# The last stage of a two-layer graph attention network, its instructions put in another order on TensorE and VectorE

## The chip, the cores and the metric

The kernel runs on one core of a Trainium2 chip. The metric is the device time of one launch in microseconds (us). Three runs of the kernel before took 2143.78, 2143.87 and 2149.99 us; their median is 2143.87 us.

## The reference

Two graph layers over 4096 nodes with 512 features each, with one adjacency matrix. The second layer is itself two rounds of attention and a dense network of two layers:

```python
def heads(x, mask, W, a):
    Wh = einsum('nf,hfo->hno', x, W)
    e = leaky_relu(src[:, :, None] + dst[:, None, :], 0.2)   # src, dst: Wh times the halves of a
    attn = softmax(where(mask, e, NEG), axis=-1)
    return einsum('hnm,hmo->hno', attn, Wh)
...
x = layernorm(x + L0(x, adj))                  # 8 heads of 64
h = elu(heads(x, adj > 0, W1, a1))             # 8 heads of 64
h2 = elu(heads(h, adj > 0, Wo, ao)[0])         # 1 head of 512
out = relu(h2 @ lin1_w + lin1_b)               # 512 -> 1024
x = layernorm(x + out @ lin2_w + lin2_b)       # 1024 -> 512
```

The adjacency is sparse (some 8 neighbours of a node on the mean, many more for the first nodes). The kernel finds the edges, and works on lists of them.

## The kernel before

The work runs in four stages: the edges are found; the attention of layer 0; the first attention of layer 1; and the last stage, which is the second attention of layer 1 together with the dense network, the residual and the norm. The change lies in the last stage alone (from L1404).

Nodes lie in 32 tiles of 128. A tile's edges are cut into chunks of 128, and chunks into units of at most 6 (GC). The last stage has 66 units, called u0 to u65 here in their order. Tiles with few neighbours have one unit or two; tile 0 has eleven (u16 to u26). Tiles are put together in blocks (L1417 to L1421): two tiles in the first block and in the last, four in each of the seven others.

What a unit needs, with the function and lines:

- **gather** (L1067): one indirect DMA for each chunk, issued by GpSimd, brings 128 rows of the table into `g`. Four units' buffers (GT) exist; unit i + 4 is gathered once unit i has been summed.
- **next weights**, `weights` (L1133): three small VectorE operations on the scores (`z`, L1147, L1148, L1150; the first waits for the gather) and an exponential on ScalarE (`w`, L1158).
- **matrices and sums**, `add` (L1160): VectorE makes a 128x64 selection matrix for each slot from `w` (`sm`, L1187), TensorE multiplies by the gathered rows into `acc` (L1212).

What a tile needs:

- **scores**, `spread` (L1078), two tiles ahead: matmuls into `pss` (L1101, L1108), a sum on VectorE (`s`, L1117) and `ls` (L1129). More than 20 chunks make several cuts, all but the last of which are collected at once.
- **the tile's end**: `inverse` (`rd`, L1224), `normal` (`o`, L1239), then `elu`: two ScalarE operations (`ex`, L1247, L1248) and one on VectorE (L1249). In `fold` all of it stands in one place.
- **the turn**, `turn` (L1447): four transposes of `o` on TensorE (L1452), and a ScalarE copy into `sht` (L1453). With the last tile of a block turned, eight dense pieces of the block become ready (four for a block of two tiles).

What a block needs: **dense pieces**. `first_dense` multiplies `sht` by `lin1_w` (L1475) and leaves relu on ScalarE (`shid`, L1478). `second_dense` loads the residual row `xr` on the SP queue (L1483), adds the bias on VectorE (L1484), multiplies `shid` by `lin2_w` (L1487), and leaves the rest for `close`: the residual (L1492), the **norm** on VectorE (L1253 to L1266) with two ScalarE operations in its middle (L1258, L1259), and the store on the SP queue (L1494). `piece` (L1459) takes the next piece from `ready`, after `close`.

The last stage is under `tc.manual_schedule()`: each engine takes its instructions in the order in which the loop emits them, and the loop's order is each engine's order. A piece is due when `due` reaches 1; `due` grows by `pace` for each chunk, so that the pieces of one block are spread over the units of the next. In the loop before, a unit emits, in this order: scores' matmuls of the tile two ahead, the turn of the tile ended one unit earlier, the next unit's weights, the earlier tile's `rd`, matrices and sums, gather, `close`, the tile's end, the scores' rest, due pieces.

Of the kernel before, what the change touches and what calls it, by code (L numbers as in the profile page):

```python
# [10 lines left out]
F32 = mybir.dt.float32  # L11
# [10 lines left out]
P = 128  # L22
N = 4096
F = 512
# [534 lines left out]
def sparse_path(  # L559
# [23 lines left out]
    nc = tc.nc  # L583
# [57 lines left out]
    x1_d = dram.tile([N, F], F32, name="sx1_d")  # L641
# [407 lines left out]
    def units_of(order):  # L1049
        units = []  # L1050
        for t in order:
            own = [
                Unit(t, [(p.first + i, n) for i, n in runs], slots)
                for p in pts if p.t == t for runs, *slots in p.units()
            ]
            own[0].first = own[-1].last = True
            units += own
        return units
# [186 lines left out]
    def elu(sb, o):  # L1245
        ex = sb.tile([P, F], F32, name="ex")
        nc.scalar.activation(ex, o, AF.Relu, scale=-1.0)  # L1247
        nc.scalar.activation(ex, ex, AF.Exp, scale=-1.0)  # L1248
        return lambda: nc.vector.scalar_tensor_tensor(o, ex, -1.0, o, op0=OP.add, op1=OP.max)  # L1249

    def layernorm(sb, y):
        bs = sb.tile([P, 6], F32, name="bs")
        nc.vector.bn_stats(bs, y)  # L1253
        mv = sb.tile([P, 2], F32, name="mv")
        nc.vector.bn_aggr(mv, bs)
        rs = sb.tile([P, 2], F32, name="rstd")
        lg, r = rs[:, 0:1], rs[:, 1:2]
        nc.scalar.activation(lg, mv[:, 1:2], AF.Ln, bias=eps)  # L1258
        nc.scalar.activation(r, lg, AF.Exp, scale=-0.5)  # L1259

        def rest():

            nc.vector.scalar_tensor_tensor(lg, mv[:, 1:2], EPS, r, op0=OP.add, op1=OP.mult)
            nc.vector.scalar_tensor_tensor(lg, lg, -0.5, r, op0=OP.mult, op1=OP.mult)
            nc.vector.scalar_tensor_tensor(r, lg, 1.5, r, op0=OP.add, op1=OP.mult)
            nc.vector.tensor_scalar(y, y, mv[:, 0:1], r, op0=OP.subtract, op1=OP.mult)  # L1266

        return rest
# [87 lines left out]
    with ExitStack() as pools:  # L1356
        big = pools.enter_context(tc.tile_pool(name="eb", bufs=1))
        sb = pools.enter_context(tc.tile_pool(name="es", bufs=2))
# [24 lines left out]
    sb = ctx.enter_context(tc.tile_pool(name="ls", bufs=2, reuse_waits="tile"))  # L1383
# [23 lines left out]
    with tc.tile_pool(name="tg", bufs=GT, side="right", reuse_waits="tile") as gp, \  # L1407
            tc.tile_pool(name="tb", bufs=1, side="right", reuse_waits="tile") as big, \
            tc.tile_pool(name="ta", bufs=2, space=PSUM, reuse_waits="tile") as pacc, \
            tc.tile_pool(name="tp", bufs=1, space=PSUM, reuse_waits="tile") as ps, tc.manual_schedule():  # L1410

        few = NT - 12
        blocks = [[NT - 1, NT - 2], [NT - 3 - i for i in range(NJ)]]
        blocks += [[1 + b, few // 2 - b, few // 2 + 1 + b, few - b] for b in range(few // NJ)]
        blocks.insert(3, [NT - 9, 0, NT - 8, NT - 7])  # L1417
        blocks.append([NT - 10, NT - 11])
        assert sorted(sum(blocks, [])) == list(range(NT))
        order = [t for block in blocks for t in block]  # L1420
        units = units_of(order)  # L1421
        at = Attention(st2, gp, wk, pacc, ps)
        for _ in range(GT):
            nc.gpsimd.memset(gp.tile([P, GC, F + HS], F32, name="g"), 0.0)
        for u in units[:GT]:
            at.gather(u)
        l1w = big.tile([P, FC, HID], F32, name="sl1w")
        nc.sync.dma_start(l1w, lin1_w.rearrange("(c p) o -> p c o", p=P))
        l2w = big.tile([P, HC, F], F32, name="sl2w")
        nc.sync.dma_start(l2w, lin2_w.rearrange("(c p) o -> p c o", p=P))  # L1430
        l1b_r = big.tile([HC, P], F32, name="sl1b_r")
        nc.sync.dma_start(l1b_r, lin1_b.rearrange("(c p) -> c p", p=P))
        l2b = big.tile([P, F], F32, name="sl2b")
        nc.sync.dma_start(l2b, lin2_b.partition_broadcast(P))
        hts, hids, ready, open_ = {}, {}, [], []

        def fold(t):
            o = at.normal(sb, t)
            elu(sb, o)()
            return o  # L1440

        def turn(t, o):
            b = next(b for b, block in enumerate(blocks) if t in block)
            j, nb = blocks[b].index(t), len(blocks[b])
            if j == 0:

                while any(r[1] == b - 2 and r[0] is first_dense for r in ready):  # L1447
                    piece()
                hts[b] = big.tile([P, FC, NB], F32, name="sht", bufs=2)
            pt = ps.tile([P, FC, P], F32, name="pt")  # L1450
            for c in range(FC):
                nc.tensor.transpose(pt[:, c, :], o[:, ts(c, P)], ident)  # L1452
            nc.scalar.copy(hts[b][:, :, ts(j, P)], pt)  # L1453
            if j == nb - 1:
                per = HC // nb
                ready.extend((first_dense, b, range(i * per, (i + 1) * per)) for i in range(nb))
                ready.extend((second_dense, b, i) for i in range(nb))

        def piece():  # L1459
            close()  # L1460
            of, *what = ready.pop(0)
            of(*what)

        def close():
            while open_:
                open_.pop(0)()

        def first_dense(b, ks):
            if 0 in ks:
                hids[b] = big.tile([P, HC, NB], F32, name="shid")  # L1470
            for k in ks:
                n = len(blocks[b]) * P
                p1 = ps.tile([P, NB], F32, name="p1", tag="p", bufs=2)[:, :n]
                for c in range(FC):
                    nc.tensor.matmul(  # L1475
                        p1, l1w[:, c, ts(k, P)], hts[b][:, c, :n], start=(c == 0), stop=(c == FC - 1)
                    )
                nc.scalar.activation(hids[b][:, k, :n], p1, AF.Relu, bias=l1b[:, k : k + 1])  # L1478

        def second_dense(b, j):  # L1480
            t = blocks[b][j]
            xr = sb.tile([P, F], F32, name="xr", bufs=3)
            nc.sync.dma_start(xr, x1_d[ts(t, P), :])  # L1483
            nc.vector.tensor_add(xr, xr, l2b)  # L1484
            p2 = ps.tile([P, F], F32, name="p2", tag="p", bufs=2)
            for k in range(HC):
                nc.tensor.matmul(  # L1487
                    p2, hids[b][:, k, ts(j, P)], l2w[:, k, :], start=(k == 0), stop=(k == HC - 1)
                )

            def rest():
                nc.vector.tensor_add(xr, p2, xr)  # L1492
                layernorm(sb, xr)()
                nc.sync.dma_start(out[ts(t, P), :], xr)  # L1494

            open_.append(rest)

        for t in order[:2]:
            at.spread(t)()
        at.weights(units[0])  # L1500
        l1b = big.tile([P, HC], F32, name="sl1b")
        pb = ps.tile([P, HC], F32, name="pt")
        nc.tensor.transpose(pb, l1b_r, ident[:HC, :HC])
        nc.vector.tensor_copy(l1b, pb)


        pace = {t: 0.0 for t in blocks[0]}
        for last, block in zip(blocks, blocks[1:]):
            chunks = sum(u.n for u in units if u.t in block)
            pace.update((t, 2 * len(last) / chunks) for t in block)  # L1510
        due, folded = 0.0, None
        for i, u in enumerate(units):
            pos = order.index(u.t)
            spread = at.spread(order[pos + 2]) if u.first and pos + 2 < NT else None
            if folded:
                turn(*folded)
                folded = None
            if i + 1 < len(units):
                at.weights(units[i + 1])
            if u.first and pos > 0:  # L1520
                at.inverse(sb, order[pos - 1])
            at.add(u)
            if i + GT < len(units):
                at.gather(units[i + GT])
            close()
            if u.first and pos > 0:
                folded = order[pos - 1], fold(order[pos - 1])
            if spread:
                spread()
            due = min(due + u.n * pace[u.t], 2.5)  # L1530
            while due >= 1 and ready:
                due -= 1
                piece()
        if folded:
            turn(*folded)
        at.inverse(sb, order[-1])
        turn(order[-1], fold(order[-1]))
        while ready:
            piece()
        close()  # L1540
# [56 lines left out]
```

## Time and profile before

| | |
|---|---|
| time of the profiled execution | 2328.89 us (its span 2326.7 us) |
| median of the three runs without a profile | 2143.87 us |
| PE (TensorE) busy | 1776.6 us, 76% |
| DVE (VectorE) busy | 1328.1 us, 57% |
| ACT (ScalarE) busy | 658.9 us, 28% |
| POOL (GpSimd) busy | 1161.8 us, 50% |
| granted TensorE clock, mean | 0.885 |
| first gather of the last stage | 1556.5 us from the span's start |
| first dense piece | 1607.2 us |

The last stage is the last 770 us of the profiled execution. In the profile's rows an engine is named first, then the line, the operation and what it writes and reads; a bracket at the end of a row of the timeline gives the idle time of that engine before it, and who ended it. A float32 matmul is recorded as two passes, so that a piece of eight matmuls is 16 records.

### The profile page before, as it was taken

The page shows a single profiled execution, that of the slowest core. Times are in us where ns is not written, and L with a number is a line of the kernel's source. Part 1 is how long each engine was busy: PE and PEld are TensorE (multiplying, and loading weights), DVE is VectorE, ACT ScalarE, POOL GpSimd, SP SyncE. Part 2 cuts the span into 40 slices and gives each one's busy share as a digit, 9 for nine tenths or more (in the row PEclk, how much of TensorE's full clock was granted, in tenths as well). Part 3 has the DMA queues.
Part 4 walks back from the last instruction along what each step waited for, and adds up shares of the span by engine and source line. Part 5 has one row for each costly group of instructions (what it writes and reads, how often), then busy time and mean ns, then how long its engine had stood idle before and what let it go on. Part 6 is the DMA issues. An engine that isn't in the chain of part 4 may idle for free.

```text
span 2326.7 us, 29282 instructions
## 1 busy us (share of the span) xinstructions
PE 1776.6 (76%) x8987; PEld 1038.4 (45%) x8987; DVE 1328.1 (57%) x3920; ACT 658.9 (28%) x2311; POOL 1161.8 (50%) x1662
## 2 busy tenths in 40 slices
PE   4778776643987775754997767746999898998997
PEld 3555442212665543531665444424445444444444
DVE  6887776744998776733777655733243424334322
ACT  3446776650332211100433221101111111121121
POOL 5424444456556664627556665646355634444300
PEclk9989997866999896875999988877999999999999
DMA  6434665525667775625566665545354524335301
GB/s 222 141 115 159 224 256 207 210 80 163 201 209 219 212 209 144 174 60 145 154 159 170 175 182 145 158 128 143 87 150 131 170 81 148 101 110 151 93 16 52
DMA packets 132589, 351.94 MB, mean 151 GB/s; under 512 B 41922, under 2 KB 42954, under 8 KB 128454
## 3 DMA queue, kind: packets, MB, share of 16 engines
q0 software_dynamic: 74160, 206.25, 33.1%
q1 hardware_dynamic: 58262, 143.72, 17.5%
q8 instruction: 74, 1.21, 0.2%
q14 instruction: 93, 0.76, 0.1%
HBM read 347.31 MB, written 42.24 MB: 167 GB/s over the span
## 4 chain that ended last, share of the span: by engine, by line
PE 36%; DVE 12%; issue 9%; another core or an unknown queue 6%; DMA 3%; POOL 3%; ACT 2%; SPq 0%; DVEq 0%; POOLq 0%; ACTq 0%
PE acc L1212 13%; PE p L1475 9%; PE ph L697 6%; PE p L1487 5%; DVE g L1200 4%; POOL g L1076 3%; DMA g<-table_t,idx 2%; DMA xr<-sx_d 1%; PE pt L683 1%; DVE bs L1253 1%; DVE sm L1179 1%; DVE sm L1187 1%; DVE xr L1492 1%; DVE z L1147 1%
## 5 line engine op out<-in xcount | busy, mean ns | idle before, releaser
L1076 POOL DMA_INDIRECT g<-table_t,idx x927 | 937.4, 1011 | 720.1 <-PE acc L1212 352.9
L1212 PE MATMUL acc<-g,sm 128*64 128x260 f32 (+2 forms) x4068 | 619.9, 424 | 219.9 <-DVE g L1200 100.7
L1212 PEld LDWEIGHTS acc<-g,sm 128*64 128x64 f32 x4068 | 347.9, 150 | 462.7 <-issue 177.8
L697 PE MATMUL ph<-sw_t,xt 128*128 128x264 f32 (+1 forms) x1536 | 408.4, 415 | 82.1 <-ACT xt L686 46.3
L697 PEld LDWEIGHTS ph<-sw_t,xt 128*128 128x128 f32 x1536 | 303.4, 204 | 154.2 <-ACT xt L686 63.0
L1200 DVE TENSOR_TENSOR g<-g,wp 128x2048 f32<-128x2048 f32 (+3 forms) x132 | 349.1, 2645 | 22.8 <-ACT wp L1155 20.2
L884 DVE MAX8 cand<-key 128x8 f32<-128x353 f32 (+55 forms) x467 | 197.3, 449 | 77.7 <-PE key L878 77.1
L1475 PE MATMUL p<-sht,sl1w 128*128 128x512 f32 (+1 forms) x576 | 229.3, 553 | 2.2 <-issue 1.2
L1487 PE MATMUL p<-sl2w,shid 128*128 128x512 f32 x512 | 227.0, 598 | 0.0
L686 ACT ACTIVATE xt<-pt 128x128 f32<-128x128 f32 x384 | 101.1, 278 | 286.5 <-PE pt L683 132.3
L710 ACT COPY hrow<-ph 128x260 f32<-128x260 f32 (+2 forms) x194 | 71.1, 373 | 311.1 <-PE ph L697 146.2
L1475 PEld LDWEIGHTS p<-sht,sl1w 128*128 128x128 f32 x576 | 107.6, 191 | 114.0 <-issue 108.7
L1487 PEld LDWEIGHTS p<-sl2w,shid 128*128 128x128 f32 x512 | 95.4, 190 | 120.1 <-issue 119.3
L1249 DVE SCALAR_TENSOR_TENSOR o<-ex,o 128x512 f32<-128x512 f32 x64 | 44.4, 694 | 182.8 <-ACT ex L1248 145.1
L877 PE MATMUL key<-sg,s_identb 128*128 128x512 bf16 (+1 forms) x258 | 111.6, 434 | 15.4 <-DVE cand L884 10.1
L848 ACT ACTIVATE sg<-raw 128x4096 bf16<-128x4096 int32 (+1 forms) x39 | 116.9, 2998 | 6.6 <-DMA raw<-in_adj_dram 3.7
L1478 ACT ACTIVATE shid<-p,sl1b 128x512 f32<-128x512 f32 (+1 forms) x72 | 46.0, 639 | 249.5 <-PE p L1475 212.0
L878 PE MATMUL key<-frac,places 128*128 128x512 bf16 (+1 forms) x258 | 111.1, 431 | 2.7 <-POOL places L784 2.7
L1187 DVE TENSOR_SCALAR sm<-iota_n,nl,w 128x64 f32<-128x64 f32 x339 | 83.1, 328 | 31.9 <-ACT w L1158 31.1
L1147 DVE TENSOR_TENSOR z<-s,g 128x16 f32<-128x16 f32 (+9 forms) x291 | 43.6, 174 | 92.0 <-DMA g<-table_t,idx 83.7
L1117 DVE TENSOR_REDUCE s<-pss 128x48 f32<-128x144 f32 (+21 forms) x108 | 32.1, 298 | 102.3 <-remote 55.1
L686 ACT ACTIVATION_READ_ACCUMULATOR xt<-pt 128x1 f32 x384 | 79.7, 208 | 0.0
(185 smaller groups left out, 1811.3 us busy)
## 6 DMA issues: line engine op xcount, KB each, us to landing
raw<-in_adj_dram SPq DMA_DIRECT2D x31, 2048.0 KB
table_t<-hrow SPq DMA_DIRECT2D x64, 260.0 KB
xr<-in_x_dram SPq DMA_DIRECT2D x64, 256.0 KB
g<-table_t,idx POOLq DMA_INDIRECT x927
table_t<-hrow SPq DMA_DIRECT2D x32, 257.0 KB
sx_d<-o SPq DMA_DIRECT2D x32, 256.0 KB
xr<-sx_d SPq DMA_DIRECT2D x32, 256.0 KB
out_dram<-xr SPq DMA_DIRECT2D x32, 256.0 KB
```

What stands on the lines that cost most here:

```text
L686: nc.scalar.activation(xt[:, c, :], pt[:, c, :], AF.Copy, accum_out=st.xparts[:, c, t : t + 1])
L697: nc.tensor.matmul(ph[:n], columns(c), st.w[:, c, j], start=(c == 0), stop=(c == FC - 1))
L848: nc.scalar.activation(sg[:, ts(i, w)], raw[:, ts(i, w)], AF.Sign)
L877: nc.tensor.matmul(out_, ident_b, sg[:, j:e], start=True, stop=False)
L878: nc.tensor.matmul(out_, places[:, w], frac[:, j - w * KW : e - w * KW], start=False, stop=True)
L884: nc.vector.max(out=cand[:, at : at + 8], in_=part)
L1076: nc.gpsimd.indirect_dma_start(out=u.g[:, k, : self.st.row], out_offset=None, in_=self.st.table[:, :], in_offset=bass.IndirectOffsetOnAxis ...
L1187: nc.vector.tensor_scalar(sm[:, at + i], of_g, node[k], u.w[:, k], op0=OP.is_equal, op1=OP.mult)
L1200: nc.vector.tensor_mul(body, body, wp[:, :, :, None].to_broadcast(body.shape))
L1212: nc.tensor.matmul(out_[g * HN : (g + 1) * HN], sm[:, slot], rows(k), start=start, stop=stop)
L1475: nc.tensor.matmul(p1, l1w[:, c, ts(k, P)], hts[b][:, c, :n], start=(c == 0), stop=(c == FC - 1))
L1487: nc.tensor.matmul(p2, hids[b][:, k, ts(j, P)], l2w[:, k, :], start=(k == 0), stop=(k == HC - 1))
```

## The change

Only the loop and the helpers of the last stage are changed; the same instructions are issued, in another order. A unit now emits: scores' matmuls; one due piece; matrices and sums; gather; the scores' rest; the turn of the tile ended one unit earlier; the earlier tile's `rd`, `o` and the two ScalarE steps of `elu`; `close`; the next unit's weights; the VectorE step of `elu`; further due pieces. `due` grows at the unit's start. A residual row is loaded when the piece before it is taken, by `rows_of`.

```diff
+            if ready and ready[0][0] is second_dense:
+                rows_of(*ready[0][1:])
             of(*what)
+
+        def rows_of(b, j):
+            t = blocks[b][j]
+            if t not in resid:
+                resid[t] = sb.tile([P, F], F32, name="xr", bufs=3)
+                nc.sync.dma_start(resid[t], x1_d[ts(t, P), :])
...
         def second_dense(b, j):
             t = blocks[b][j]
-            xr = sb.tile([P, F], F32, name="xr", bufs=3)
-            nc.sync.dma_start(xr, x1_d[ts(t, P), :])
+            rows_of(b, j)
+            xr = resid.pop(t)
...
             spread = at.spread(order[pos + 2]) if u.first and pos + 2 < NT else None
-            if folded:
-                turn(*folded)
-                folded = None
-            if i + 1 < len(units):
-                at.weights(units[i + 1])
-            if u.first and pos > 0:
-                at.inverse(sb, order[pos - 1])
+            due = min(due + u.n * pace[u.t], 2.5)
+            if due >= 1 and ready:
+                due -= 1
+                piece()
             at.add(u)
             if i + GT < len(units):
                 at.gather(units[i + GT])
-            close()
-            if u.first and pos > 0:
-                folded = order[pos - 1], fold(order[pos - 1])
             if spread:
                 spread()
-            due = min(due + u.n * pace[u.t], 2.5)
+            if folded:
+                turn(*folded.pop(0))
+            last, rest = units[i - 1].t if u.first and i else None, None
+            if last is not None:
+                at.inverse(sb, last)
+                o = at.normal(sb, last)
+                rest = elu(sb, o)
+            close()
+            if i + 1 < len(units):
+                at.weights(units[i + 1])
+            if rest:
+                rest()
+                folded.append((last, o))
             while due >= 1 and ready:
                 due -= 1
                 piece()
-        if folded:
-            turn(*folded)
-        at.inverse(sb, order[-1])
-        turn(order[-1], fold(order[-1]))
+        last = order[-1]
+        at.inverse(sb, last)
+        o = at.normal(sb, last)
+        elu(sb, o)()
+        for what in folded + [(last, o)]:
+            turn(*what)
```

How it stands on TensorE where the fifth block's last tile (tile 19, u36 and u37) gives way to the next block's first (tile 3, u38 to u40), read from the order of the two programs' instructions:

```
before: turn of 12, sums u37, dense | scores, sums u38 | turn of 19, sums u39, dense
after:  dense, sums u37, turn of 12 | scores, sums u38 | sums u39, turn of 19, dense
```

Units whose sums follow the sums of the unit before with no dense piece between them, from u7 on: before 7, 10, 14, 19, 21, 23, 25, 27, 30, 35, 39, 48, 57, 65; after 7, 9, 13, 16, 18, 20, 22, 24, 26, 29, 30, 34, 38, 39, 47, 48, 56, 57, 64, 65. The last tile of a block is turned in u3, u7, u16, u30, u39, u48, u57 and u65, before and after; after, the turn stands behind that unit's sums, and the block's first dense piece directly behind the turn.

More of the change, by code (lines that the diff above doesn't have):

```diff
@@ L1434, in sparse_path @@
         nc.sync.dma_start(l2b, lin2_b.partition_broadcast(P))
[L1435 to L1440, printed above, removed]
+        hts, hids, resid, ready, open_ = {}, {}, {}, [], []
         def turn(t, o):
@@ L1510, in sparse_path @@
             pace.update((t, 2 * len(last) / chunks) for t in block)
-        due, folded = 0.0, None
+        due, folded = 0.0, []
         for i, u in enumerate(units):
```

## The prediction

> **What bounds the kernel now.** I read the page's slices first, then the busy time by stretches, the waits of the last stage, and the timeline. The slices (58 us each) show the last stage from the 27th on:
>
> ```profile
> PE   4778776643987775754997767746999898998997
> PEclk9989997866999896875999988877999999999999
> ```
>
> TensorE is filled to eight or nine tenths there, at a granted clock of nine tenths. The busy time by stretches narrows it (length, then PE, PEld, DVE, ACT, POOL, clock, DMA share, GB/s):
>
> ```profile
> 1660.00:1720.00 60.00, 59.74 (x228) 29.89 (x226) 16.93 (x70) 9.47 (x20) 29.09 (x30) 0.97 0.41 114
> 1900.00:1960.00 60.00, 50.91 (x214) 24.57 (x212) 26.37 (x96) 8.44 (x23) 26.10 (x27) 0.97 0.41 120
> ```
>
> The first stretch, with a piece in nearly every unit, is full; the second, with units that have none (u34, u38), loses 9 us in 60, and DVE is under half busy. So the stage is worth TensorE's work plus its holes, and only holes can be won or lost. The timeline shows a typical one (u47 and u48, tile 18 ending a block):
>
> ```profile
> 2042.31 0.96 DVE L1187 TENSOR_SCALAR sm<-iota_n,nl,w 128x64 f32<-128x64 f32 x4
> ...
> 2043.04 2.02 PE L1212 MATMUL acc<-g,sm 128*64 128x257 f32 x16
> 2043.19 0.69 DVE L1492 TENSOR_TENSOR xr<-p,xr 128x512 f32<-128x512 f32 x1
> ...
> 2046.47 0.74 DVE L1239 TENSOR_SCALAR o<-acc,rd 128x512 f32<-128x512 f32 x1
> ...
> 2047.24 0.63 ACT L1247 ACTIVATE ex<-o 128x512 f32<-128x512 f32 x1 [1.86 <-DVE o L1239]
> ...
> 2048.57 0.69 DVE L1249 SCALAR_TENSOR_TENSOR o<-ex,o 128x512 f32<-128x512 f32 x1 [1.36 <-ACT ex L1248]
> ...
> 2049.31 1.05 PE L1452 MATMUL pt<-s_ident,o 128*128 128x128 f32 x4 [4.26 <-issue]
> ...
> 2050.43 3.35 PE L1212 MATMUL acc<-g,sm 128*64 128x257 f32 x16
> ```
>
> With no piece left, TensorE waits 4.26 us for the turn of `o`, which on VectorE stands behind a whole norm. Then the turn takes 1.05 (0.60 elsewhere) and the sums 3.35 (1.95 elsewhere). The stage's start is different; there the gathers rule:
>
> ```profile
> 1572.05 0.17 DVE L1147 TENSOR_TENSOR z<-s,g 128x5 f32<-128x5 f32 x1 [5.95 <-DMA g<-table_t,idx]
> ...
> 1572.90 5.85 PE L1212 MATMUL acc<-g,sm 128*64 128x257 f32 x24 [21.02 <-DMA g<-table_t,idx]
> ```
>
> VectorE waits for u1's gather before it makes the matrices of u0, whose scores were ready at 1565.40. Last, one line of the waits:
>
> ```profile
> DVE xr L1484 <- DMA xr<-sx_d: 56.1, 17, 5.5
> ```
>
> **What the Trainium skill says.** "TensorE: Matmul & The Clock Gate", Part 1 (the HAM clock gate): TensorE falls to half clock after an idle window of some 3.4 us and recovers after as long a busy one. The trace agrees in size: after holes of 3.65 us the turn ran at a granted 0.50, and 24 passes of sums took 5.4 us for 2.82; but a hole of 2.42 also brought 0.61, and one of 2.55 nothing. The same page (engine queue depths) has ScalarE and VectorE strictly in order; the trace fits, with `ex` at 1634.26 queued behind four `shid`, a copy and `w`, although `o` was done at 1627.54. "Perfetto Trace Analysis" (Tensor Engine Instruction) says that a matmul's end is an estimate. Here `rd` at 1835.4 waited for sums whose record ends at 1832.1: true ends can be 3 us later.
>
> **The change part by part.** Prices, all from the timeline of before: piece 7.0 on PE (16 passes of 0.436); sums of a 4-chunk unit 1.95, of a 6-chunk unit 2.82, at half clock some 4.0 and 5.4; turn 0.6, its copy starting 0.64 after the turn and holding ACT 0.48; matrices: first sums 0.36 after their start, 0.98 or 1.43 in all; norm from the last matmul: 0.20, then 1.67 to the mean and variance, ACT 0.56, three small operations 0.6, the last 0.47; weights 0.65, `w` 0.25; `rd` and `o` 0.95, both `ex` 1.31, elu's end 0.6; scores' rest 0.4.
>
> Same instructions, so TensorE's work is unchanged. Where a piece precedes the sums (most units), its 7.0 us cover the chain from one unit's sums to the next: the longest is some 8.5 (worked out below) against 2.82 + 0.6 + 0.3 + 7.0 = 10.7, so moving it costs nothing there; without the piece it costs what follows.
>
> *Uncovered units.* The next weights now stand at the unit's end, behind turn copy (ACT), norm and tile's end. Take u38, from the end of u37's piece: sums u37 to 1.95, turn and scores to 2.85. The copy holds ACT from 2.59 to 3.07; only then come the norm's two operations (mean ready at 1.87): to 3.63; norm done 4.70, weights 5.35, `w` 5.60, first sums 5.96. Hole 3.1, where before had 1.45. The added wait is the copy's: queued behind it are the norm's operations and `w`, and VectorE and TensorE wait for those. Then u39, from u38's sums: matrices done 0.62, rest 1.02, `o` 1.97, `ex` 3.31, elu's end 3.9, sums 4.27, against 1.95 of work: 2.3, mostly hidden if the clock is halved. Last, the piece right behind the turn waits for the copy: 0.7. Together 6.4; before this place lost 8.8 (1.45 + 4.25 in holes, 3.1 in slow passes).
>
> The same working gives, in us lost after / before: u7 8.3 / 8.2; u29 and u30 11.6 / 6.9 (one-unit tiles: copy, both `ex`, norm and `w` in a row make 8.46 to the sums, hole 4.8, then 2.3 and two slow sums); u34 and u35 4.6 / 6.5 (3.1, and 60% of a cold start of 2.5); u38, u39 6.4 / 8.8; u47, u48 6.4 / 6.1; u56, u57 6.4 / 7.5; u64, u65 6.5 / 3.6. New holes: u13 4.7 / 0 (norm, weights, elu to 5.1 against sums of 1.95, then the same), u16 8.0 / 0 (4.8, cold 2.5, copy 0.7), u18 1.3 / 0. In tile 0, u24 and u26 4.8 / 11.0 (before: 2.42 and 3.42 in holes, 5.2 in slow passes; u9, u20, u22 are free, 2.3 against 2.8). Its scores' cuts 3.0 / 5.1 (no matrices to wait for behind them). Tail: 3.8 / 5.3. Short waits of sums on matrices elsewhere, before, 5.6 (five of 0.4 to 1.2, and first passes at 134 for 106 ns); after, none.
>
> Sums: after 75.8, before 74.6: **1.2 us lost**.
>
> *Loading rows early* (SP queue): DVE's 56 us at L1484 vanish. The load moves past no store that it needs; the store before it waits for VectorE either way, three buffers serve. That gain is in the short waits and 1 us of the tail already; the rest was idle beside a running piece.
>
> *The start.* u0's sums no longer wait for u1's gather, and so on for each: one gather of six chunks, 6 x 1.30 = 7.8 us, earlier to the first piece. GpSimd issues without a break there, so nothing else is late at once. Bounds: 0, if what delayed the first turn's copy (done on PE at 1584.0, on ACT at 1598.3, released by nothing that the trace names) comes back; 15, as the gather of u3 would allow a first piece at some 1592 against 1607.2. I take 7.8. Scaled by 2143.87 / 2328.89 = 0.92, as issue seems slower under the profile: 7.2. Holes of TensorE I carry over one to one.
>
> Net: 2328.9 - 7.8 + 1.2 = 2322.3 for a profiled execution, 2143.9 - 7.2 + 1.2 = **2138** for the median.
>
> **The rivals.** *Slower.* True ends of matmuls are late. The new chains pass through TensorE's end (copy) and its last piece (norm) before the next sums, which the old order avoided by having `w` a unit ahead. With 2 us (the trace has 1.5, `rd` at 1705.7 behind a record's end at 1704.2, and 3.3 at 1835.4) at eight places (u7, u13, u16, u29, u34, u38, u47, u56) it is 16 us: 2138 + 16 = 2154. It decides once it costs more than 5.9 / 8 = 0.7 us a place. For it: these two waits; against: ordinary copies start 0.04 us after the record's end. *Faster.* The start yields its 15 us (14 scaled), and half the holes, 3.1 us being below the skill's window, don't cool the clock (five of 2 us, half of them): 2143.9 - 14 + 1.2 - 5 = 2126. For it: the hole of 2.55; against: that of 2.42. *No gain at the start*: the unexplained wait returns; 2143.9 + 1.2 = 2145. That the order isn't as written is excluded by the built program.
>
> **How the numbers follow.** Forecast (2132 to 2143) 0.40; faster 0.20; no gain 0.15; slower 0.25. A difference of 0.3% (6.4 us) is about what a measurement of this kernel can tell from no change. The forecast lies on that edge: half of it counts as faster, 0.20 + 0.20 = 0.40; the other half and two thirds of no gain are the same, 0.30; the rest slower, 0.30. The range leaves out a tenth on either side: 2124, a little below the faster rival, to 2157, a little above the slower one.
>
> **What would show it.** Right: the sums of u0 near 1567 instead of 1572.9, the first piece some 8 us earlier; no wait of L1484 on its DMA; no hole ahead of a turn, but holes of 3 to 5 us ahead of the sums of u13, u16, u29, u34, u38, u47 and u56, ended by VectorE's matrices, with the copy, the norm's two operations and `w` in a row on ScalarE. Wrong: such holes missing (or over 6 us), holes in units that a piece covers, or a start that is no earlier.

## The result, and the profile after

The changed kernel takes 2143.01 us (median of 20 runs, 2136.8 to 2148.05) against 2142.44 us (20 runs, 2138.2 to 2149.99) for the kernel before on the same chip: ratio 1.0004, 95% interval 0.9996 to 1.0012. It makes no difference that can be told. The prediction was 2138 in a range of 2124 to 2157.

One fact is needed for the numbers that follow: the chips differ. The kernel before takes some 2142 us on the chip of this result, and 2317 or 2334 us on two others that were used. A chip on which it takes some 2142 us is called short here, one of the others long. The profile in the section on the time before (2328.9 us) came, by its time, from a long chip, the profile of the changed kernel (2146.34 us, span 2144.1) from a short one. A ratio here is always of runs on one chip. So that the two profiles could be compared, the kernel before was profiled again on a short chip: 2145.92 us, span 2143.6. "Before" means that profile from here on, except where the longer one is named.

The slices of the changed kernel (53.6 us each; the last stage begins in the 26th):

```profile
PE   4877777663888886857999777578989899999998
PEclk9999998786999998978999988789999999999999
```

TensorE is filled to eight or nine tenths in the last stage, as before. The busy time by stretches shows what moved. Each stretch below runs from the first dense piece of a block to that of the next, and the eighth, which takes in the ninth block, to the span's end; columns are the stretch, its length, then PE, PEld, DVE, ACT and POOL busy with their instructions, the granted clock, the DMA share and GB/s. First the kernel before, then the changed one:

```profile
1435.80:1487.90 52.10, 47.01 (x237) 30.81 (x236) 21.77 (x88) 11.23 (x26) 24.06 (x24) 0.93 0.48 138
1487.90:1578.90 91.00, 87.32 (x403) 42.74 (x402) 33.85 (x125) 15.87 (x37) 44.92 (x45) 0.98 0.44 127
1578.90:1690.00 111.10, 105.06 (x460) 52.90 (x458) 46.16 (x193) 16.58 (x42) 68.92 (x68) 0.97 0.56 159
1690.00:1784.40 94.40, 83.10 (x327) 39.91 (x326) 34.43 (x130) 15.86 (x37) 38.94 (x38) 0.95 0.39 114
1784.40:1870.50 86.10, 81.19 (x334) 39.69 (x333) 33.37 (x129) 15.65 (x37) 38.50 (x38) 0.98 0.41 116
1870.50:1960.30 89.80, 83.86 (x350) 41.57 (x349) 32.91 (x126) 15.67 (x37) 41.02 (x40) 0.98 0.44 128
1960.30:2042.70 82.40, 79.85 (x332) 38.73 (x331) 33.39 (x118) 16.71 (x37) 22.31 (x22) 1.00 0.30 84
2042.70:2143.60 100.90, 85.97 (x233) 43.71 (x232) 21.24 (x51) 14.38 (x32) 0.00 (x0) 0.94 0.09 30
```

```profile
1429.20:1479.80 50.60, 44.57 (x236) 29.65 (x236) 20.46 (x76) 12.23 (x29) 29.86 (x30) 0.93 0.58 160
1479.80:1579.10 99.30, 89.94 (x401) 44.97 (x401) 37.53 (x142) 15.83 (x38) 45.71 (x45) 0.95 0.43 122
1579.10:1698.70 119.60, 106.75 (x458) 55.52 (x458) 43.45 (x179) 16.86 (x43) 69.03 (x69) 0.96 0.51 143
1698.70:1787.30 88.60, 81.34 (x325) 38.70 (x325) 33.51 (x128) 15.68 (x38) 35.77 (x35) 0.96 0.39 112
1787.30:1874.80 87.50, 82.46 (x334) 39.80 (x334) 33.96 (x130) 15.89 (x38) 39.49 (x39) 0.96 0.41 120
1874.80:1961.70 86.90, 82.87 (x348) 40.67 (x348) 34.88 (x134) 15.83 (x38) 41.59 (x42) 0.98 0.45 130
1961.70:2046.80 85.10, 80.85 (x331) 38.55 (x331) 33.69 (x120) 15.79 (x37) 22.60 (x23) 0.98 0.30 87
2046.80:2144.10 97.30, 85.51 (x232) 43.88 (x232) 21.45 (x52) 15.50 (x34) 0.00 (x0) 0.96 0.08 28
```

Look at the first number of each row and at the lengths. The first piece comes 6.6 us earlier (1429.2 for 1435.8); both kernels begin the last stage at the same moment (first gather at 1390.8 in the changed one, 1390.7 before). Then the second and the third stretch lose 8.3 and 8.5 us, the fourth and the last win 5.8 and 3.6, and the others balance: 7.1 us lost in all from the first piece to the end (714.9 against 707.8), so that the span ends 0.5 us later.

The start, as the timeline of the changed kernel has it (start, duration, engine, line, operation, tiles; in brackets the idle time before, and who ended it):

```profile
1400.93 5.49 PE L1212 MATMUL acc<-g,sm 128*64 128x257 f32 x24 [14.77 <-DVE sm L1187]
...
1406.32 0.17 DVE L1147 TENSOR_TENSOR z<-s,g 128x5 f32<-128x5 f32 x1 [3.91 <-DMA g<-table_t,idx]
...
1409.04 0.75 DVE L1239 TENSOR_SCALAR o<-acc,rd 128x512 f32<-128x512 f32 x1
...
1413.48 0.17 DVE L1147 TENSOR_TENSOR z<-s,g 128x5 f32<-128x5 f32 x1 [3.69 <-DMA g<-table_t,idx]
```

The sums of u0 begin at 1400.93, before VectorE's wait for u1's gather (1406.32) instead of behind it; before, they begin at 1407.35. The tile's `o` also stands ahead of the next wait for a gather. u47 and u48, the place shown of the kernel before, look like this now:

```profile
1861.57 0.58 ACT L1448 COPY sht<-pt 128x512 f32<-128x512 f32 x1 [7.36 <-PE pt L1447]
1862.05 0.30 ACT L1258 ACTIVATE rstd<-mv,s_eps 128x1 f32<-128x1 f32 x1
...
1864.56 0.21 ACT L1158 ACTIVATE w<-z 128x4 f32<-128x4 f32 x1 [1.98 <-DVE z L1150]
1864.80 0.98 DVE L1187 TENSOR_SCALAR sm<-iota_n,nl,w 128x64 f32<-128x64 f32 x4 [0.27 <-ACT w L1158]
...
1865.17 3.28 PE L1212 MATMUL acc<-g,sm 128*64 128x257 f32 x16 [3.53 <-DVE sm L1187]
```

The hole of 4.26 us ahead of the turn is gone. In its place TensorE waits 3.53 us for matrices, behind the copy of the turn, the norm (`rstd`) and `w`, one after the other. Last, the waits (us in total, times, longest). First the kernel before, on `xr` and on `w`, then the changed one on the same two:

```profile
DVE xr L1484 <- DMA xr<-sx_d: 66.7, 22, 5.3
DVE sm L1187 <- ACT w L1158: 31.8, 5, 16.6
```

```profile
DVE xr L1488 <- DMA xr<-sx_d: 3.2, 1, 3.2
DVE sm L1187 <- ACT w L1158: 146.2, 27, 19.8
```

Of 22 waits for a row one is left, in the tail (2113.74). VectorE waits for `w` instead.

### The profile page after: what moved, and what is told of

The parts are those of the page before. It is cut to its first block, busy times and chain, and to the rows that moved or that the text cites. A ratio compares the mean times of both kernels' runs of the same rounds, so it can differ in the third digit from the quotient of the medians.

```text
span 2144.1 us, 29259 instructions
## 1 busy us (share of the span) xinstructions
PE 1719.4 (80%) x8987; PEld 1008.6 (47%) x8987; DVE 1327.8 (62%) x3920; ACT 662.0 (31%) x2311; POOL 1164.6 (54%) x1662
## 4 chain that ended last, share of the span: by engine, by line
PE 36%; DVE 12%; issue 8%; DMA 8%; POOL 7%; ACT 2%; POOLq 0%; DVEq 0%; ACTq 0%; SPq 0%
PE acc L1212 11%; PE p L1479 11%; PE p L1491 10%; DMA g<-table_t,idx 7%; POOL g L1076 6%; DVE g L1200 4%; PE ph L697 3%; DVE sm L1179 1%; PE pt L1447 1%; DVE o L1232 1%; DVE z L1147 1%; DVE z L1150 1%; DVE z L1148 1%; ACT sht L1448 1%; DVE sm L1187 1%
## 5 line engine op out<-in xcount | busy, mean ns | idle before, releaser
L1212 PE MATMUL acc<-g,sm 128*64 128x260 f32 (+2 forms) x4068 | 583.5, 420 | 221.2 <-DVE g L1200 151.8
L1212 PEld LDWEIGHTS acc<-g,sm 128*64 128x64 f32 x4068 | 336.0, 149 | 463.8 <-DVE g L1200 180.0
L697 PE MATMUL ph<-sw_t,xt 128*128 128x264 f32 (+1 forms) x1536 | 395.5, 405 | 46.2 <-ACT xt L686 40.5
L697 PEld LDWEIGHTS ph<-sw_t,xt 128*128 128x128 f32 x1536 | 294.1, 198 | 113.7 <-ACT xt L686 60.5
L884 DVE MAX8 cand<-key 128x8 f32<-128x353 f32 (+55 forms) x467 | 196.5, 446 | 79.2 <-PE key L878 78.6
L1496 DVE TENSOR_TENSOR xr<-p,xr 128x512 f32<-128x512 f32 x32 | 22.1, 692 | 132.6 <-PE p L1491 132.6
L1155 ACT ACTIVATE wp<-z 128x32 f32<-128x32 f32 (+3 forms) x132 | 27.2, 206 | 199.7 <-DVE g L1200 199.6
```

The costliest lines, as they stand in the source:

```text
L697: nc.tensor.matmul(ph[:n], columns(c), st.w[:, c, j], start=(c == 0), stop=(c == FC - 1))
L884: nc.vector.max(out=cand[:, at : at + 8], in_=part)
L1212: nc.tensor.matmul(out_[g * HN : (g + 1) * HN], sm[:, slot], rows(k), start=start, stop=stop)
```

## The experiments

**The kernel before, three times more.** One unused name is added, so the program is the same. It was profiled on each of the three chips used for the experiments.

```diff
         due, folded = 0.0, None
+        early = ()
```

> The kernel before once more, for a second profile: that of the forecast has a span of 2326.7 us where the median without a profile is 2142.4, while the changed kernel's profile has 2144.1. Forecast's theory (the change brings 7 us at the start and nothing in the holes): this profile shows the first dense piece some 49 us after the stage's first gather against 41 in the changed kernel (53.6 in the first profile), and from there on to the end about what the changed kernel takes, 715 us. Rival (no gain at the start, since what delayed the first turn's copy belongs to the first profile alone): the first piece comes 41 to 43 us after the first gather, and the rest takes 715 too. Third theory (the start gains and the rest loses it): 49 us to the first piece, and 707 after it.

> The kernel before once more, on the chip of the three runs beside it, for a profile that can be held against theirs. The last stage took 773 us in both profiles so far, on a chip where the whole kernel takes 2334 us; in the changed kernel's profile (2144 us) it took 756. Forecast's theory: on a chip of 2142 us the stage of the kernel before takes about 756 too, with the first dense piece 49 us after the first gather and 707 from there to the end. Rival (the start gives nothing, the holes are even): 41 and 715.

> The kernel before once more, for a profile of it on the chip of this call. Both theories expect the span's stages as in the earlier profiles of before, with the last stage's holes on TensorE near 48 us and its sums near 182 us. If the chip is one on which the kernel takes some 2140 us, the theory that the longer last stage of the other chips is extra delay between TensorE's instructions expects the stage from its first dense piece to its end at 705 to 716 us here instead of 719 to 721; the theory that the kernel's holes alone set that stretch expects 719 to 721.

Measured: 2325.97, 2321.69 and 2145.92 us. In the last stage, the part from the first piece to the span's end takes 720.9, 718.9 and 707.8 us: the last lies where the theory of added delay put it (705 to 716), not where holes alone would (719 to 721). Its holes on TensorE behind the first piece come to 43 us, though, where both theories had 48. The expectations count the first piece from the clearing of the last gather buffer, 2.9 us before the first gather. By that count it comes after 48.0 us on the short chip, so that the third theory of the first run holds: the start gains, and the rest loses it. The difference between the chips sits early in the part behind the first piece. The third stretch of the long profile shown before the prediction stands against 111.10 us above:

```profile
1754.70:1872.80 118.10, 108.58 (x459) 56.50 (x457) 46.64 (x196) 16.57 (x42) 67.83 (x68) 0.93 0.53 149
1872.80:1967.60 94.80, 83.20 (x326) 39.96 (x325) 33.88 (x127) 15.85 (x37) 38.94 (x38) 0.95 0.39 113
1967.60:2053.70 86.10, 81.41 (x334) 40.07 (x333) 33.20 (x129) 15.64 (x37) 38.49 (x38) 0.98 0.41 116
```

In the fourth and fifth stretch that profile agrees with the short one within 0.4 us; in the third, which is mostly tile 0, it takes 7.0 us more (the other two long profiles: 118.5 and 118.0). The first stretch takes 4.3 to 5.2 us more on the long chips.

**The changed kernel on a long chip.** The program is the same but for such a name.

> The changed kernel again, beside the kernel before on this chip. If the chip is like that of the comparison (2142 us), ratio 1.000. If it is one of 2334 us, the theory that the early rows bring 16 us there (ratio 0.993 for them alone) expects 0.993 to 0.995 with the forecast's even holes; the rival, that the new order loses what the rows bring, expects 1.000 there as well.

Measured: 2339.29 against 2316.88 us, ratio 1.0084 (1.0061 to 1.0106). There the change is a loss. The first piece comes 55.3 us after the stage's first gather (before on that chip 51.2, changed on the short chip 38.5), the second and third stretch take 107.2 and 126.3 us, and from the fourth on every stretch is within 0.2 us of the table above. The timeline shows what such a chip adds, here in the scores of a tile with several cuts:

```profile
1725.07 0.20 DVE L1117 TENSOR_REDUCE s<-pss 128x12 f32<-128x36 f32 x1 [8.67 <-remote]
1725.31 0.19 PE L1101 MATMUL pss<-hole,s_identb 128*128 128x39 bf16 x1 [6.16 <-issue]
...
1729.37 0.20 DVE L1117 TENSOR_REDUCE s<-pss 128x13 f32<-128x39 f32 x1 [4.10 <-remote]
1729.62 0.19 PE L1101 MATMUL pss<-hole,s_identb 128*128 128x39 bf16 x1 [3.90 <-DVE s L1117]
```

Both engines stand idle for 4 to 9 us, and three of the four waits are put down to "remote" or "issue", which name no instruction of the program. On the short chip TensorE has holes of 0.29 us in the same place. Why is open: no run here reaches the cause.

**The start alone**, in the kernel before: for the first three units the next weights stand behind the sums.

```diff
-            if i + 1 < len(units):
-                at.weights(units[i + 1])
+            if i >= 3:
+                at.weights(units[i + 1]) if i + 1 < len(units) else None
...
             at.add(u)
+            if i < 3:
+                at.weights(units[i + 1])
```

> The kernel before, in which units 0 to 2 alone make the next unit's weights behind their own matrices and sums, as the changed kernel does. Forecast's theory: 7 us faster than before (ratio 0.997). Rival, no gain at the start: within 1 us, as the first piece waits for something else.

Measured on a long chip: 2336.31 against 2334.44 us, ratio 1.0007 (0.9994 to 1.0019): no gain. The last run below has the same edit on a short chip, and its trace shows where the gain is lost.

**The early rows alone**, in the kernel before, on a long chip and again on a short one.

```diff
+            if ready and ready[0][0] is second_dense:
+                rows_of(*ready[0][1:])
...
-            xr = sb.tile([P, F], F32, name="xr", bufs=3)
-            nc.sync.dma_start(xr, x1_d[ts(t, P), :])
+            rows_of(b, j)
+            xr = resid.pop(t)
```

> The kernel before, with the residual rows loaded one piece early, as in the changed kernel, and nothing else of it. Forecast's theory: the waits at L1484 (56 us on VectorE) vanish, of which TensorE felt 4 to 6 us (short waits of sums on matrices, the hole of 1.45 us at u38, 1 us in the tail): ratio 0.997 to 0.998. Rival (all of it lay beside running pieces): ratio 1.000.

> The kernel before with the rows loaded early, on the chip of this call. Theory: the load keeps VectorE from making the next unit's matrices in time, and is worth 10 to 16 us on any chip (ratio 0.992 to 0.996). Rival: it is worth what the prediction counted in short waits and in the tail, at most 6.6 us (ratio 0.997 to 1.0). The order alone and the rows alone should multiply to the changed kernel's ratio within 0.3% if the two parts do not meet.

Measured: ratio 0.993 (0.9917 to 0.9943) on the long chip; 2128.62 against 2142.41 us on the short one, ratio 0.9931 (0.9912 to 0.995). That is 14 us, not the 6.6 that the prediction counted. The ratio is the same on both kinds of chip; the first of these runs had theories of 0.997 and above, which both fall.

**The order alone**: the changed kernel without its early rows.

```diff
-            if ready and ready[0][0] is second_dense:
-                rows_of(*ready[0][1:])
```

> The changed kernel with a residual row loaded when its own piece is taken, as in the kernel before: the order alone. Theory: the order alone is a loss, which the early rows pay back in part or in full. Where the early rows are worth 16 us and the change 0.8% slower, the order alone is 1.5% slower than before (ratio 1.013 to 1.018); on a chip where the change is even with before, 0.4 to 0.8% slower. Rival, the prediction's own sum: rows early are worth nearly nothing on their own and the order loses 1 us, so that this kernel is at the changed kernel's ratio, within 0.2% of it.

Measured, on the same short chip: 2166.28 us, ratio 1.0113 (1.0093 to 1.0133). The order alone is 24 us slower than before. The size expected for a chip on which the change is even (0.4 to 0.8%) was too small, and the prediction's sum (within 0.2% of the changed kernel) fails. The two parts as ratios make 1.0113 x 0.9931 = 1.0043, against 1.0004 for the change, outside the 0.3% named; the intervals of the two parts reach 0.2% to either side each. One place of this kernel shows how a late row costs TensorE:

```profile
1764.30 0.38 SPq L1464 DMA_DIRECT2D xr<-sx_d  x1
...
1768.82 0.69 DVE L1486 TENSOR_TENSOR xr<-xr,sl2b 128x512 f32<-128x512 f32 x1 [4.38 <-DMA xr<-sx_d]
1769.43 0.98 DVE L1187 TENSOR_SCALAR sm<-iota_n,nl,w 128x64 f32<-128x64 f32 x4
...
1769.79 2.39 PE L1212 MATMUL acc<-g,sm 128*64 128x257 f32 x16 [1.08 <-DVE sm L1187]
```

The row is asked for at 1764.30 and lands at 1768.8; VectorE stands for 4.38 us ahead of the matrices, although `w` was done at 1764.67; and 1.08 us of it outlast the running piece. Such a hole, between 0.8 and 2.2 us, ends seven pieces of this kernel from u30 on; the changed kernel has none.

From the first piece to the span's end the four kernels take, in us:

| | rows late | rows early |
|---|---|---|
| order of before | 707.8 | 692.9 |
| order of the change | 730.4 | 714.9 |

The order costs 22.6 or 22.0, the rows win 14.9 or 15.5: in these four executions, behind the first piece, the two parts add up. For the whole kernel the medians leave some 10 us open (24 lost and 14 won, against 0.6), and single executions of one kernel lie up to 13 us apart.

The four traces also say how well the start is known. From the first gather to the first piece they take 45.2 us (before), 43.5 (rows alone), 38.5 (the change) and 40.1 (order alone). The rows play no part up to there, so two traces of one order differ by 1.6 us by themselves; the new order gains 3.4 to 6.7 us there, 5.0 on the mean.

**Pieces at a slower pace**, in the changed kernel.

```diff
-            pace.update((t, 2 * len(last) / chunks) for t in block)
+            pace.update((t, 0.8 * 2 * len(last) / chunks) for t in block)
```

> The changed kernel with the pace of the dense pieces cut to 0.8, so that pieces are left at a block's end to stand between the sums there. Theory that the changed kernel's holes are uncovered units: those of u7, u16, u29, u34, u38, u47, u56 and u64 (2.8 to 5 us each with their copies, some 35 us in all with slow passes) mostly vanish, the pieces left over lengthen the tail only by their own work: 20 to 35 us faster than the changed kernel (ratio to before 0.985 to 0.99). Rival (VectorE's chain, not the missing piece, sets the pace at the ends of blocks): within 5 us.

Measured on a long chip: ratio 1.004 (1.0023 to 1.0056), with 57.3 us of holes between the first piece and the end. Pieces only came later (the second stretch grew to 127.8 us, the seventh shrank to 61.1). The changed kernel itself wasn't run on that chip, so this run doesn't settle what a piece in the gap is worth. Its ratio lies above the 0.985 to 0.99 of the theory.

**One piece in each gap between sums**, first in the order of the change, then in the order of before with early rows. A piece is dealt to nearly every unit; in tile 0 to every second one. The second kernel asks the same for the next unit, at a unit's end.

```diff
-            due = min(due + u.n * pace[u.t], 2.5)
-            if due >= 1 and ready:
-                due -= 1
+            long_ = sum(p.n for p in parts_of(u.t)) > 30 and not u.first
+            here = [v.t for v in units[max(i - 4, 0) : i]]
+            third = len(here) == 4 and here[0] != here[1] == here[2] == here[3]
+            take = i % 2 and ready and ready[0][0] is first_dense if long_ else not third
+            if ready and take:
                 piece()
...
-            while due >= 1 and ready:
-                due -= 1
-                piece()
```

> The changed kernel with the pieces dealt out anew: one ahead of each unit's sums as long as one is ready, none at a unit's end; passed over only behind a third unit of a tile and in most of tile 0. Then u7, u13, u16, u29, u30, u34, u38, u39, u47, u48, u56, u57, u64 and u65 all have a piece ahead of their sums. Theory (a unit without a piece costs the chain of copy, norm, weights; a piece covers it): the losses of those units go, 8.3 + 4.7 + 8.0 + 11.6 + 4.6 + 3 x 6.4 + 6.5 + 4.8 in tile 0 = 68 us, less 5 for copies right behind turns: some 60 us faster than the changed kernel, ratio to before 0.972. Rival (VectorE or the gathers set the pace of a unit, and the holes move): under 15 us faster, ratio over 0.993.

> The kernel before in its old order, with the early rows and with the pieces dealt out as in the run just named (a piece behind one unit stands ahead of the next). If it is the missing piece that costs, whatever the order, this order gains as much: ratio 0.970 to 0.975, even a little better as no piece stands right behind a turn. If the new order is what makes a covered unit cheap, it stays 10 us or more behind that run.

Measured on one long chip: 2289.15 us, ratio 0.9863 (0.9831 to 0.9894), in the order of the change, and 2273.02 us, ratio 0.9807 (0.9784 to 0.983), in the order of before. Both gains are smaller than expected (0.972, and 0.970 to 0.975). In the order of the change the piece in the gap wins 2339.29 - 2289.15 = 50 us, nearer to the theory's 60 than to the rival's 15. With it the two orders still differ, by 0.6%, but no longer in the middle of the stage: the fourth to sixth stretch take 78.7, 79.5 and 81.3 us in one and 78.4, 79.2 and 81.0 in the other, with no hole over 0.7 us. Of the 14.4 us between the two spans, 11.7 lie ahead of the first piece. So there it is the missing piece that makes either order cost time.

**The best with the start**: the last of these with the edit of the start alone.

> The order of the kernel before, rows early, one piece dealt to each gap between sums, and the next weights of the first three units behind the sums, as the change has it. One piece a gap alone gave a ratio of 0.981. Theory: the start is worth nothing or little, ratio 0.979 to 0.983, with the first sums some 6 us earlier but the first piece at 50 to 55 us from the stage's first gather. Rival, the prediction's 7 us: ratio 0.976 to 0.978 and the first piece at 42 to 47 us.

Measured on the short chip: 2095.2 us, ratio 0.9783 (0.9762 to 0.9804), 47 us faster than either kernel. The ratio fits either theory. The first piece comes 43.6 us after the first gather (46.5 by the count of the expectation), which is where the rival had it; but the rows alone, without the edit, have it after 43.5. So this start earns nothing, though u0's sums begin at 1400.79, as early as in the change. The trace shows where the gain goes:

```profile
1413.46 0.74 DVE L1239 TENSOR_SCALAR o<-acc,rd 128x512 f32<-128x512 f32 x1
...
1417.52 5.42 PE L1212 MATMUL acc<-g,sm 128*64 128x257 f32 x24
...
1428.54 0.17 DVE L1147 TENSOR_TENSOR z<-s,g 128x6 f32<-128x6 f32 x1 [4.62 <-DMA g<-table_t,idx]
...
1429.46 4.81 PE L1212 MATMUL acc<-g,sm 128*64 128x257 f32 x24 [4.95 <-DVE sm L1187]
```

Two places give it back. The weights stand behind the sums but ahead of the tile's `o`, so `o` waits for a gather (1413.46 for 1409.04 in the change), and u2's sums (1417.52), behind the turn of `o`, are late by 2.6 us. The larger loss comes one unit on. The edit ends with u2: u3's matrices stand again behind u4's weights, and VectorE waits until 1428.54 for u4's gather. So u3's sums begin at 1429.46, in the rows alone at 1429.48, in the change at 1423.51; and the first piece stands behind them. The edit is thus one unit too short to test the prediction's start, here and in the run of the start alone; a kernel with the edit for four units was not run.

In the middle of the stage nothing is left to win in two stretches:

```profile
1674.70:1753.10 78.40, 78.14 (x328) 37.62 (x326) 32.95 (x126) 15.54 (x37) 38.18 (x38) 1.00 0.48 137
1753.10:1832.30 79.20, 78.94 (x335) 38.14 (x333) 33.93 (x130) 15.54 (x37) 38.21 (x38) 1.00 0.45 127
```

These are the stretches that took 94.40 and 86.10 us before, and 88.60 and 87.50 with the change: TensorE is busy all but 0.26 us, and the clock is full. The stretch before them, mostly tile 0, keeps one hole of 8.27 us (1627.23), behind VectorE's wait of 9.49 us for a gather.

## Why the prediction was right, and where it was not

The forecast lay 5 us low, within its range. It gave "the same" a chance of 0.30 and "faster" 0.40. That the total came so near is luck in part, as two errors of opposite sign stand in it. Its steps:

**The start: right in mechanism, at the upper end in size.** 7.2 us were forecast. The two traces above have 6.6 in the first piece and 6.4 in u0's sums; the four traces of both orders have 3.4 to 6.7 in the first piece. The rival "no gain at the start" (2145) came nearer to the number, but for a wrong reason: the gain is there, and is lost later.

**The holes: right in place and size.** Forecast and measured in us: u13 3.1 and 2.87; u16 4.8 and 4.93; u18 1.3 and 1.13; u29 4.8 and 4.91; u30 2.3 and 2.82; u34 3.1 and 3.26; u38 3.1 and 3.35; the copy ahead of a block's first piece 0.7 and 0.67. The hole of u39 was to be hidden by slow sums: there is none, and the sums of u38 took 4.13 us for 1.95. The others foreseen of 3 to 5 us, u47 and u56, have 3.53 and 3.36. One sum is off: the terms given for u38 (3.1, 2.3 and 0.7) make 6.1, not 6.4, which over the three places that take it is 0.9 us. The rival "slower" needed 2 us more at each of eight places and falls. The waits that it rested on were misread: the long profile puts those of `rd` at 1705.7 and 1835.4 down to "remote" and not to the sums, and on the short chip `rd` of the second place starts at 1656.20, with the record of its sums ending at 1656.17. So it isn't shown that matmuls end 3 us after their record.

**The sum of the losses: the failed step.** It said 75.8 us after against 74.6 before, 1.2 lost; 7.1 were. By stretches (rows early from the experiment of the rows alone):

| stretch, and what the prediction put there | forecast change | before | before, rows early | changed | measured change |
|---|---|---|---|---|---|
| 1: u7 | +0.1 | 52.1 | 48.3 | 50.6 | -1.5 |
| 2: u13, u16, the scores' cuts | +10.6 | 91.0 | 89.0 | 99.3 | +8.3 |
| 3: u18, u24 and u26, u29 and u30 | -0.2 | 111.1 | 111.3 | 119.6 | +8.5 |
| 4: u34, u35, u38, u39 | -4.3 | 94.4 | 91.4 | 88.6 | -5.8 |
| 5: u47, u48 | +0.3 | 86.1 | 85.5 | 87.5 | +1.4 |
| 6: u56, u57 | -1.1 | 89.8 | 86.4 | 86.9 | -2.9 |
| 7: u64, u65 | +2.9 | 82.4 | 83.1 | 85.1 | +2.7 |
| 8: tail | -1.5 | 100.9 | 97.9 | 97.3 | -3.6 |
| short waits, in no one stretch | -5.6 | | | | |
| sum | +1.2 | 707.8 | 692.9 | 714.9 | +7.1 |

Without the third stretch the forecast is 1.2 + 0.2 = +1.4 and the measured change 7.1 - 8.5 = -1.4, which is 2.8 us better; the third stretch alone is 8.7 us worse. The term mis-sized is "tile 0 (u24, u26) 4.8 / 11.0": the 11.0 of before were holes of 2.42 and 3.42 us and 5.2 in slow passes, read from the long profile. On the short chip the hole of 3.42, ahead of u27, doesn't exist, and u25's sums lose a hole of 2.37 and 4.02 - 1.95 = 2.1 us in slow passes, 4.5 together. So 6.5 us of before, which the change was to save, were not there to be saved; they are most of the 7.0 us by which that chip was longer in this stretch. The rest lies in u29 and u30: 12.7 us after (holes of 4.91 and 2.82, sums of 5.94 and 4.70 for 2.82 each) for the 11.6 of the forecast, and a hole before of 2.81 for 3.65.

**The scale of 0.92: a wrong reason.** "As issue seems slower under the profile" does not hold: the changed kernel's profiled execution took 2146.34 us, inside the 2136.8 to 2148.05 of all its runs. The 2328.9 us were, by the time, another chip. The step moved the number by only 0.6 us, but the mismatch of 9% was the warning that the losses of before might be those of another chip as well.

**The early rows: mis-sized, and hidden by the order.** "That gain is in the short waits and 1 us of the tail already; the rest was idle beside a running piece" is refuted: 14 us alone, not 6.6. The table shows where it went: into stretches 1, 2, 4, 6 and 8, partly inside holes that the prediction had put down to the order. So the order's own cost came out too small as well: without the 6.6 us of the rows (5.6 in short waits, 1 in the tail) the sum forecasts 7.8 us for the order from the first piece on, and it costs 22. In the four traces the rows won 8 us more than forecast and the order lost 14 more; that the one hides most of the other is luck.

**The clock.** The Trainium skill's "TensorE: Matmul & The Clock Gate", Part 1 (the HAM clock gate), has an idle window of some 3.4 us ahead of half clock. The two short profiles agree for their holes above 3.3 us, which bring slow sums; but before, the hole of 2.37 us ahead of u25 was followed by 16 passes in 4.02 us for 1.95, so the forecast was right not to count on a limit.

What stays open: why some chips add idle time to TensorE early in the stage. It is shown that they do, and that the change loses 0.8% on the one long chip on which it ran, where it loses nothing on the short one; the cause isn't. Each chip was measured at one time only, so that a chip and its condition at that time can't be told apart. Open too are the 10 us by which the medians of the two parts miss the whole.

## What to carry to other kernels

When a profiled execution and the runs without a profile are 9% apart, find out first whether they are the same kind of machine: every loss read from the profile may belong to the other. An edit with two parts is priced as two parts: here early rows that win 14 us alone hid an order that loses 24 alone, and the better of the two parts alone beat the whole. Where a unit's chain is longer than its work on the bound engine, shortening or reordering the chain moves a hole from one place to the next; one piece of independent work in every gap removed it in the middle of the stage, in either order.

## What the runs showed of the hardware that was not expected

- Three chips, each measured at one time, run one and the same program in some 2142, 2317 and 2334 us, yet from the fourth stretch of the last stage on within 1.7 us a stretch; the difference lies in the stages before (the last stage's first gather comes at 1390.7 us on the short chip, at 1556.5 in the long profile of before) and in the first part of the last.
- A row load of 256 KB, issued when it is needed, landed 4.5 us later; in the kernel before such loads kept VectorE idle 22 times, for up to 5.3 us. Loaded one piece earlier, one wait of 3.2 us was left.
- After a hole of 2.37 us 16 passes of sums took 4.02 us, at a granted clock of 0.57; after one of 3.26 us they took 2.39 us, at a granted 1.00.
